# A gated recurrence over 512 steps: a block of probe instructions placed behind the last step

## The chip, the cores and the metric

The kernel runs on one core of one Trainium2 chip. The metric is the device time of one execution in microseconds; lower is better. Within the core, TensorE multiplies matrices (in the profile PE, and PEld for its weight loads), VectorE (DVE), ScalarE (ACT) and GpSimd (POOL) work elementwise, and SyncE (SP) issues transfers.

## The reference

For each of 512 time steps, with a state `h` of 8 rows by 512 and an input `x_t` of the same shape:

```python
def step(h, x_t):
    fused = sigmoid(concatenate([x_t, h], -1) @ w_W + w_b)
    hidden_state, output_state = split(fused, 2, -1)
    memory_state = x_t @ wx_W + wx_b + hidden_state * (h @ wh_W + wh_b)
    h_new = output_state * h + (1.0 - output_state) * tanh(memory_state)
    return h_new, h_new
out = x + scan(step, cond_1024, x)
```

Everything is float32. Step t+1 needs the `h` of step t, so the 512 steps run one behind the other.

## The kernel before

The 512 units of the state lie as 128 partitions by 4 chunks. All weights stay in SBUF: `wx` (line 118) for the input's part, `wgr` (line 122) and `whh` (line 125) for the state's part. `head` (line 92) holds the first half chunk of x and the first state. The order of instructions is the order of the program text (`tc.manual_schedule()`, line 170); on each engine they run in that order, and semaphores carry the dependences between engines.

Each step `i` of the loop at line 258 does this:

- TensorE, through the helper `mm` (line 177; every product has line 178 in the profile): 48 products of the state with the weights, each a fp32 stationary of 128x32 and a moving operand of 128x128, in the order of `ORDER` (line 27). The four output quarters `32*j` are taken in turn, so that four products run side by side in the four column groups of the array. The results add up in the PSUM banks R, G and H. Then `take(later, 1)` issues a quarter of the input's products for a coming group of four steps (`prefill`, line 215), into one of the two PSUM tiles `xps` (line 175).
- VectorE: 32x32 block transposes out of the banks (`turned`, line 301, recorded at line 303; `turn_h`, line 320), scans that form the gate sums and the new state (`scans`, line 280), and three one-column memsets of `idle` (line 383).
- ScalarE: sigmoids and tanh (`act`, line 204), and the copies that spread the input's part into the banks (`spread`, line 227) and write the bias (`seed`, line 211).
- GpSimd: the residual sum into `ot` (`add`, line 384), and SyncE: the store of 16 steps at a time (`store`, line 392).

The last step stands apart (lines 400 to 403): GpSimd adds one half (line 361), VectorE adds the other (`add(1, nc.vector)`, recorded at line 385), and SyncE stores the last four steps (line 395). Nothing follows.

Of the kernel before, what the change touches and what calls it, by code (L numbers as in the profile page):

```python
# [7 lines left out]
F32 = mybir.dt.float32  # L8
BF16 = mybir.dt.bfloat16
AF = mybir.ActivationFunctionType  # L10
ALU = mybir.AluOpType
PSUM = bass.MemoryType.PSUM

P = 128
NQ = 4
# [21 lines left out]
def tile_cond_rnn_residual(  # L37
# [39 lines left out]
    nc = tc.nc  # L77
# [4 lines left out]
    const = ctx.enter_context(tc.tile_pool(name="const", bufs=1))  # L82
# [9 lines left out]
    head = const.tile([P, NX + NQ * B], F32, name="head")  # L92
# [12 lines left out]
    def x_of(c, k, t, n):  # L105

        e, t = divmod(t, TC // 2)
        if c == 0 and e == 0:
            first = head[:, :NX].rearrange("p (k n) -> p k n", k=NQ)
            return first[:, k, t * B : (t + n) * B]  # L110
        return xins[c][:, e, k, t * B : (t + n) * B]
# [6 lines left out]
    wx = const.tile([P, NQ, NQ, 384], F32, name="wx")  # L118
# [6 lines left out]
    whh = const.tile([P, NQ, NQ, 128], F32, name="whh")  # L125
# [22 lines left out]
    zeros = const.tile([P, 512], F32, name="zeros")  # L148
# [14 lines left out]
    idle = const.tile([P, IDLE], F32, name="idle")  # L163

    def state(hf, i, slot=2):

        s = i % GS
        return hT[hf][i % NH][:, B * s : B * s + B, :, slot]
# [6 lines left out]
    xps = [psum.tile([P, 512], F32, name=f"xp{q}") for q in range(2)]  # L175

    def mm(out_, lhsT, rhs, start=False):
        nc.tensor.matmul(  # L178
            out_, lhsT, rhs, start=start, stop=False, skip_group_check=True
        )  # L180
# [11 lines left out]
    bias = const.tile([P, 512], F32, name="bias")  # L192
# [65 lines left out]
    for i in range(T):  # L258
        g, s = divmod(i, GS)
        c, t = divmod(i, TC)  # L260
# [6 lines left out]
        for n in (ORDER if i else FIRST).split():  # L267
# [3 lines left out]
            bank, k = n[0], int(n[1])  # L271
# [112 lines left out]
        def add(hf, engine):  # L384
            return engine.tensor_tensor(  # L385
                ot[:, t, 2 * hf : 2 * hf + 2, :].rearrange("p c n -> p n c"),
                x_of(c, slice(2 * hf, 2 * hf + 2), t, 1).rearrange("p c n -> p n c"),
                state(hf, i + 1),
                ALU.add,
            ).ins  # L390

        def store(t0):

            n = NQ * B
            nc.sync.dma_start(
                out=out[c][:, n * t0 : n * (t + 1)],
                in_=ot[:, t0 : t + 1].rearrange("p t k b -> p (t k b)"),
            )

        if i == T - 1:  # L400
            add(1, nc.vector)
            store(TC - LAST)
            continue
        for hf in (1, 0):
# [77 lines left out]
```

## Time and profile before

| what | value |
|---|---|
| times of the two runs | 1693.63 and 1693.91 us, median 1693.77 us |
| span of the profiled execution | 1691.7 us |
| what lies around the span, against the two runs | 1.93 to 2.21 us, 2.07 us against the median |
| PE busy | 1680.3 us, 99% of the span |
| DVE busy | 1087.0 us, 64% |
| ACT busy | 915.5 us, 54% |
| POOL busy | 231.2 us, 14% |
| last DMA issue on SP | at 1689.14 us, for 0.33 us |
| `out_dram<-ot` of 192 KB and 256 KB, issue to landing | 1.9 and 3.3 us |

The profiled execution's own time outside the profiler isn't listed apart from these runs; its span stands beside them, and the difference is taken as what lies around it. A group's line in the profile gives the engine, the operation, the tiles out<-in, the shape, how often it ran, the busy time and the mean of one in ns, and the idle time of the engine ahead of it. The timeline gives start, duration, engine, operation and how many instructions are merged into a line.

### The profile page before, as it was taken

The page shows a single profiled execution, that of the slowest core. Times are in us where ns is not written, and L with a number is a line of the kernel's source. Part 1 is how long each engine was busy: PE and PEld are TensorE (multiplying, and loading weights), DVE is VectorE, ACT ScalarE, POOL GpSimd, SP SyncE. Part 2 cuts the span into 40 slices and gives each one's busy share as a digit, 9 for nine tenths or more (in the row PEclk, how much of TensorE's full clock was granted, in tenths as well). Part 3 has the DMA queues.
Part 4 walks back from the last instruction along what each step waited for, and adds up shares of the span by engine and source line. Part 5 has one row for each costly group of instructions (what it writes and reads, how often), then busy time and mean ns, then how long its engine had stood idle before and what let it go on. Part 6 is the DMA issues. An engine that isn't in the chain of part 4 may idle for free.

```text
span 1691.7 us, 121258 instructions
## 1 busy us (share of the span) xinstructions
PE 1680.3 (99%) x53230; PEld 1467.6 (87%) x53230; DVE 1087.0 (64%) x8229; ACT 915.5 (54%) x5121; POOL 231.2 (14%) x1032
## 2 busy tenths in 40 slices
PE   8999999999999999999999999999999999999998
PEld 6888888888888888888888888888888888888887
DVE  5666666666666666666666666666666666666666
ACT  3555555555555555555555555555555555555554
POOL 0111111111111111111111111111111111111111
PEclk9999999999999999999999999999999999999999
DMA  4000000000000000000000000000000000000000
GB/s 177 17 17 5 17 17 17 17 4 17 17 17 17 4 17 17 17 17 13 9 18 17 17 17 4 17 17 17 17 5 17 17 17 17 4 17 11 11 11 10
DMA packets 11483, 30.86 MB, mean 18 GB/s; under 512 B 1220, under 2 KB 1732, under 8 KB 10952
## 3 DMA queue, kind: packets, MB, share of 16 engines
q1 hardware_dynamic: 10800, 22.94, 3.9%
q8 instruction: 416, 6.82, 1.7%
q14 instruction: 115, 0.94, 0.2%
q10 hardware_dynamic: 152, 0.16, 0.0%
HBM read 14.70 MB, written 8.39 MB: 14 GB/s over the span
## 4 chain that ended last, share of the span: by engine, by line
PE 98%; DMA 1%; DVE 0%; ACT 0%; issue 0%; SPq 0%
PE R L178 26%; PE G L178 26%; PE H L178 26%; PE xp L178 19%; DMA whh<-in_whh_dram 1%; DMA head<-in_xh_dram 0%; DVE md1A L321 0%; DVE hTA L283 0%; ACT hd0A L205 0%; ACT hTA L205 0%; SPq L124 0%; DVE tz L303 0%; ACT hTB L205 0%; DVE hTB L283 0%; ACT hd0B L205 0%
## 5 line engine op out<-in xcount | busy, mean ns | idle before, releaser
L178 PE MATMUL xp<-wx,xin 128*32 128x384 f32 x4032 | 431.3, 486 | 0.0
L178 PEld LDWEIGHTS R<-wgr,hTA 128*32 128x32 f32 x8176 | 247.4, 135 | 206.8 <-DVE hTA L283 206.4
L303 DVE STREAM_TRANSPOSE tr<-R 128x64 f32<-128x64 f32 x1022 | 194.4, 229 | 309.1 <-PE R L178 309.1
L178 PE MATMUL R<-wgr,hTA 128*32 128x128 f32 x8176 | 330.9, 273 | 2.2 <-DVE hTA L283 2.2
L178 PE MATMUL H<-whh,hTA 128*32 128x128 f32 x8192 | 331.3, 273 | 0.8 <-DMA whh<-in_whh_dram 0.8
L178 PE MATMUL H<-whh,hTB 128*32 128x128 f32 x8192 | 331.2, 273 | 0.0
L178 PE MATMUL R<-wgr,hTB 128*32 128x128 f32 x8176 | 330.6, 273 | 0.0
L178 PE MATMUL G<-wgr,hTB 128*32 128x128 f32 x8176 | 330.6, 273 | 0.0
L178 PE MATMUL G<-wgr,hTA 128*32 128x128 f32 x8176 | 330.6, 273 | 0.0
L385 POOL TENSOR_TENSOR ot<-xin,hTB 128x16 f32<-128x16 f32 x503 | 126.4, 251 | 1415.6 <-DVE hTB L283 1324.0
L205 ACT ACTIVATE hd0B<-tz 128x16 f32<-128x16 f32 x512 | 114.9, 224 | 305.3 <-DVE tz L303 305.3
L205 ACT ACTIVATE md0A<-tr 128x16 f32<-128x16 f32 x512 | 119.6, 234 | 265.2 <-DVE tr L303 265.2
L178 PEld LDWEIGHTS H<-whh,hTA 128*32 128x32 f32 x8192 | 260.2, 136 | 1.2 <-DMA whh<-in_whh_dram 1.2
L178 PEld LDWEIGHTS G<-wgr,hTA 128*32 128x32 f32 x8176 | 259.8, 136 | 0.0
L178 PEld LDWEIGHTS H<-whh,hTB 128*32 128x32 f32 x8192 | 254.5, 122 | 0.0
L178 PEld LDWEIGHTS G<-wgr,hTB 128*32 128x32 f32 x8176 | 254.1, 122 | 0.0
L178 PEld LDWEIGHTS R<-wgr,hTB 128*32 128x32 f32 x8176 | 245.2, 122 | 0.0
L283 DVE TENSOR_TENSOR_SCAN hTA<-hd0A,hTA 128x48 f32<-128x48 f32 x512 | 132.1, 258 | 149.2 <-ACT hTA L205 149.2
L283 DVE TENSOR_TENSOR_SCAN hTB<-hd0B,hTB 128x24 f32<-128x24 f32 x1024 | 158.1, 196 | 104.0 <-ACT hTB L205 104.0
L205 ACT ACTIVATE hd0A<-tz 128x16 f32<-128x16 f32 x512 | 118.9, 232 | 111.4 <-DVE tz L303 111.4
L321 DVE STREAM_TRANSPOSE md1A<-G 128x64 f32<-128x64 f32 x511 | 156.8, 307 | 28.7
L205 ACT ACTIVATE hTB<-hTB 128x16 f32<-128x16 f32 x512 | 121.2, 237 | 81.1 <-DVE hTB L283 80.5
(62 smaller groups left out, 1680.2 us busy)
## 6 DMA issues: line engine op xcount, KB each, us to landing
xin<-in_x_dram SPq DMA_DIRECT2D x31, 256.0 KB, 3.8
out_dram<-ot SPq DMA_DIRECT2D x31, 256.0 KB, 3.3
wx<-in_wx_dram SPq DMA_DIRECT2D x4, 768.0 KB, 7.2
wgr<-in_wgr_dram SPq DMA_DIRECT2D x4, 512.0 KB, 9.7
whh<-in_whh_dram SPq DMA_DIRECT2D x1, 768.0 KB
whh<-in_wh_dram SPq DMA_DIRECT2D x1, 256.0 KB, 11.2
out_dram<-ot SPq DMA_DIRECT2D x1, 192.0 KB, 1.9
head<-in_xh_dram ACTq DMA_DIRECT2D x1, 144.0 KB, 5.2
```

The lines of the kernel that those rows point to most:

```text
L178: nc.tensor.matmul(out_, lhsT, rhs, start=start, stop=False, skip_group_check=True)
L205: inst = nc.scalar.activation(out_, in_, func, **kw).ins
L283: nc.vector.tensor_tensor_scan(*[t_[:, :, c_].rearrange("p n c s -> p (n c s)") for t_ in (out_, d0, d1)], 0.0, ALU.mult, ALU.add,)
L303: inst = nc.vector.transpose(t_.rearrange("p c n -> p (c n)"), raw[n][hf]).ins
L321: nc.vector.transpose(md1[hf][g % 2][:, :, :, 0].rearrange("p n c -> p c n"), raw["h"][hf])
L385: return engine.tensor_tensor(ot[:, t, 2 * hf : 2 * hf + 2, :].rearrange("p c n -> p n c"), x_of(c, slice(2 * hf, 2 * hf + 2), t, 1).rearr ...
```

## The change

A function `measure()` is defined in the loop body and called once, in the last step, behind `add(1, nc.vector)` and ahead of `store`. It issues, in this order:

- VectorE: two copies of `whh` into the bf16 tile `bw` (1536 elements in each partition, the first 384 of a chunk repeated four times) and one copy of 96 elements of `head` into `st`. `top` and `top2` are views of `st` as bf16, 24 columns each.
- TensorE: nine groups of products into `xps`, with a one-column VectorE copy out of PSUM (`bar`) behind each: 120 bf16 products of 24 stationary columns (24 + 24 + 24 of width 128, 16 of width 64, 16 of 256, 16 of 384), 16 fp32 of 8 stationary columns and width 64, 16 of width 128, and 16 fp32 of full 128x128 by 128.
- VectorE: three memsets of 640 columns; 15 transposes from PSUM in five output layouts; 6 reductions, 9 scans and 6 small elementwise operations in threes; a chain of six dependent operations.
- ScalarE: six operations; GpSimd: three; then six VectorE operations that read what these two wrote, the last into `idle`.

None of its results reach the output. `rep` and `parts` are defined and not called. A built program's instruction lists show the new rows of every engine behind all of its rows of the loop, and the rows in front unchanged; SyncE's rows stay as they were, and the last store waits for the same GpSimd and VectorE sums. The bf16 products stand as a weight load and a product, two instructions each; a fp32 product is one instruction. No further table load is on ScalarE. Line numbers from 404 on are those of the changed kernel.

```diff
+        def measure():
+            bw = const.tile([P, 2, NQ, 384], BF16, name="bw")
+            for k in range(2):
+                nc.vector.tensor_copy(bw[:, k], whh[:, k, :, :].rearrange("p j n -> p (j n)")[:, :384].unsqueeze(1).broadcast_to([P, NQ, 384]))
+            st = const.tile([P, 96], F32, name="bst")
+            nc.vector.tensor_copy(st, head[:, :96])
+            top = st[:, :72].bitcast(BF16)[:, 5:144:6]
+            top2 = st[:, :72].bitcast(BF16)[:, 1:48:2]
+            a_, b_ = xps
...
+            def bar(t_):
+                nc.vector.tensor_copy(idle[:, :1], t_[:, :1])
+            def part(k, j, p, n=128, w=1):
+                return bw[:, k, j, n * p : n * (p + w)]
...
+            for k in range(2):
+                for j in range(NQ):
+                    for p in range(3):
+                        mm(b_[32 * j : 32 * j + 24, 0:128], top, part(k, j, p), start=k + p == 0)
+            bar(b_)
+            for k in range(2):
+                for p in range(3):
+                    for j in range(NQ):
+                        mm(a_[32 * j : 32 * j + 24, 0:128], top, part(k, j, p), start=k + p == 0)
+            bar(a_)
+            for p in range(3):
+                for k in range(2):
+                    for j in range(NQ):
+                        mm(b_[32 * j : 32 * j + 24, 0:128], top2, part(k, j, p))
+            bar(b_)
+            for k in range(2):
+                for n in range(2):
+                    for j in range(NQ):
+                        mm(a_[32 * j : 32 * j + 24, 0:64], top, part(k, j, n, 64))
+            bar(a_)
...
+                        mm(b_[32 * j : 32 * j + 24, 0:256], top, part(k, j, 0, 128, 2))
...
+                        mm(a_[32 * j : 32 * j + 24, 0:384], top, bw[:, k, j])
...
+                        mm(b_[32 * j : 32 * j + 8, 0:64], st[:, 0:24:3], whh[:, k, j, :64])
...
+                        mm(a_[32 * j : 32 * j + 8, 0:128], st[:, 0:24:3], whh[:, k, j, :128])
+            bar(a_)
+            for k in range(2):
+                for j in range(NQ):
+                    for n in range(2):
+                        nc.tensor.matmul(b_[:, 0:128], wx[:, k, j, :128], wx[:, k, j, 128:256], start=False, stop=False, skip_group_check=True)
+            bar(b_)
+            u = const.tile([P, 640], F32, name="bu")
+            nc.vector.memset(u, 0.0)
...
+            V = nc.vector
+            tp = a_[:, 0:64]
+            for _ in range(3):
+                V.transpose(v[:, 0:64], tp)
+            for _ in range(3):
+                V.transpose(v[:, 0:80].rearrange("p (c b s) -> p c s b", c=2, s=5)[:, :, :4], tp)
+            for _ in range(3):
+                V.transpose(v[:, 0:80].rearrange("p (c b s) -> p c b s", c=2, s=5)[:, :, :, :4], tp)
+            for _ in range(3):
+                V.transpose(v[:, 0:80].rearrange("p (s c b) -> p c s b", c=2, s=5)[:, :, :4], tp)
+            for _ in range(3):
+                V.transpose(v[:, 0:128], a_[:, 0:128])
+            for _ in range(3):
+                V.tensor_reduce(w_[:, 0:16], v[:, 0:80].rearrange("p (c s b) -> p c b s", c=2, s=5), mybir.AxisListType.X, ALU.add)
+            for _ in range(3):
+                V.tensor_reduce(w_[:, 0:32], v[:, 0:160].rearrange("p (c s b) -> p c b s", c=4, s=5), mybir.AxisListType.X, ALU.add)
+            for _ in range(3):
+                V.tensor_tensor_scan(w_[:, 0:80], u[:, 0:80], v[:, 0:80], 0.0, ALU.mult, ALU.add)
...
+            for _ in range(3):
+                V.tensor_tensor(w_[:, 0:48:3], u[:, 0:48:3], v[:, 0:48].bitcast(BF16)[:, 1:96:6], ALU.subtract)
+            V.tensor_tensor(w_[:, 0:16], u[:, 0:16], v[:, 0:16], ALU.mult)
+            V.tensor_tensor(w_[:, 16:32], w_[:, 0:16], v[:, 0:16], ALU.mult)
+            V.tensor_tensor(w_[:, 32:48], w_[:, 16:32], v[:, 0:16], ALU.mult)
+            V.tensor_tensor_scan(w_[:, 64:112], u[:, 0:48], w_[:, 0:48], 0.0, ALU.mult, ALU.add)
+            V.tensor_tensor(w_[:, 128:144], w_[:, 64:80], v[:, 0:16], ALU.mult)
+            V.tensor_reduce(w_[:, 144:160], w_[:, 128:144].unsqueeze(2).broadcast_to([P, 16, 4]), mybir.AxisListType.X, ALU.add)
+            nc.scalar.activation(u[:, 256:288].rearrange("p (c b) -> p c b", c=4), w_[:, 0:128].rearrange("p (c n) -> p c n", c=4)[:, :, :8], AF.Sigmoid)
+            nc.scalar.activation(u[:, 288:304], w_[:, 0:16], AF.Tanh)
+            nc.scalar.activation(u[:, 320:352], w_[:, 0:32], AF.Sigmoid)
+            nc.scalar.activation(u[:, 352:480], a_[:, 0:128], AF.Identity, bias=zeros[:, :1])
+            nc.scalar.copy(b_[:, 0:128], zeros[:, 0:128])
+            nc.scalar.copy(b_[:, 0:64], zeros[:, 0:64])
+            nc.gpsimd.tensor_tensor(u[:, 512:528], w_[:, 0:16], v[:, 0:16], ALU.mult)
...
+            nc.vector.tensor_tensor(w_[:, 0:64], u[:, 256:320], u[:, 512:576], ALU.mult)
...
+            nc.vector.tensor_tensor(idle[:, :1], w_[:, 72:73], zeros[:, :1], ALU.add)
+
         if i == T - 1:
             add(1, nc.vector)
+            measure()
             store(TC - LAST)
             continue
```

## The prediction, made before the run

> **What bounds the kernel now.** I read the page first, then the end of the timeline, since the change sits behind the last step, then the groups for durations, and last the start of the timeline, the only place with bf16 products and a long idle of TensorE.
>
> ```profile
> span 1691.7 us, 121258 instructions
> ```
>
> ```profile
> PE 98%; DMA 1%; DVE 0%; ACT 0%; issue 0%; SPq 0%
> ```
>
> The first line is the span; the second, from the chain of work that ended last, gives TensorE 98% of it. The loop is TensorE's time, and the change touches no row in it. What matters is what stands behind TensorE at the end:
>
> ```profile
> 1686.48 0.62 PE L178 MATMUL H<-whh,hTA 128*32 128x128 f32 x16
> 1686.73 0.31 DVE L321 STREAM_TRANSPOSE md1A<-G 128x64 f32<-128x64 f32 x1
> 1686.92 0.62 PE L178 MATMUL H<-whh,hTB 128*32 128x128 f32 x16
> 1687.08 0.22 DVE L283 TENSOR_TENSOR_SCAN m<-md0A,md1A 128x32 f32<-128x32 f32 x1
> ...
> 1688.88 0.19 DVE L385 TENSOR_TENSOR ot<-xin,hTB 128x16 f32<-128x16 f32 x1
> 1689.14 0.33 SPq L395 DMA_DIRECT2D out_dram<-ot  x1
> ```
>
> TensorE is done at 1687.54. VectorE's last work ends at 1688.88 + 0.19 = 1689.07. The store is issued at 1689.14, and the span ends at 1691.7, so the last 2.6 us are the store alone. The scan m at 1687.08 waits for md1A, a VectorE result that ends at 1687.04: a VectorE instruction that depends on one before it starts about 0.04 to 0.06 us behind its end. I use 0.05.
>
> The groups that give prices (lines picked from all over the list of groups, shapes kept apart):
>
> ```profile
> L283 DVE TENSOR_TENSOR_SCAN hTA<-hd0A,hTA 128x48 f32<-128x48 f32 x512 | 132.1, 258 | 149.2 <-ACT hTA L205 149.2
> L283 DVE TENSOR_TENSOR_SCAN m<-md0A,md1A 128x32 f32<-128x32 f32 x512 | 115.0, 225 | 0.0
> L321 DVE STREAM_TRANSPOSE md1B<-H 128x64 f32<-128x64 f32 x512 | 115.7, 226 | 0.4 <-PE H L178 0.4
> L235 DVE STREAM_TRANSPOSE md1B<-xp 128x32 f32<-128x32 f32 x256 | 49.1, 192 | 0.0
> L160 DVE MEMSET hTA<- 128x192 f32 x8 | 1.7, 218 | 0.0
> L193 DVE COPY bias<-xp 128x512 f32<-128x512 f32 x1 | 0.7, 692 | 1.3 <-PE xp L178 1.3
> L149 DVE MEMSET zeros<- 128x512 f32 x1 | 0.5, 485 | 0.1
> L196 DVE COPY hTB<-head 128x16 f32<-128x16 f32 x2 | 0.3, 176 | 0.0
> L321 DVE STREAM_TRANSPOSE md1A<-xp 128x64 f32<-128x64 f32 x1 | 0.3, 255 | 0.0
> L385 DVE TENSOR_TENSOR ot<-xin,hTB 128x16 f32<-128x16 f32 x1 | 0.2, 189 | 0.0
> ```
>
> Scans cost (258 - 225)/16 = 2.06 ns a column, memsets (485 - 218)/320 = 0.834. And TensorE's timeline, its start and a stretch near the end:
>
> ```profile
> 2.15 0.31 PE L178 MATMUL G<-none 128*128 128x128 bf16 x1
> 2.26 0.31 PE L178 MATMUL H<-none 128*128 128x128 bf16 x1
> 2.69 3.52 PE L178 MATMUL xp<-zeros 128*128 128x512 f32 x4
> 6.77 1.10 PE L178 MATMUL xp<-rows,ones 128*128 128x512 f32 x2 [0.57 <-DVE hTB L160]
> ```
>
> ```profile
> 1661.47 0.86 PE L178 MATMUL xp<-wx,xin 128*32 128x384 f32 x8
> 1662.12 0.65 PE L178 MATMUL R<-wgr,hTA 128*32 128x128 f32 x16
> ```
>
> After 2.07 us of idle, bf16 products of 128 columns start 0.107 us apart, and fp32 records of 512 columns take 3.52/4 = 0.88; from 6.77 on, two of them fit in 1.10. So the array starts at half its later rate, though the granted clock of those windows reads 1.00.
>
> **The change part by part.** Nothing is removed or moved; SP's and the loop's rows stay. The block is behind VectorE's sum of line 385 and no earlier: TensorE's first new weight load waits for a VectorE copy that stands behind that sum, and ScalarE's and GpSimd's first new rows wait for VectorE too. So the block starts at 1689.07, beside the store. The store waits for the sum alone and is covered: its 2.6 us is no longer the end.
>
> *Copies* (on the path: TensorE waits). 1536 columns by the memset slope, since that row too stays in SBUF: 218 + 1344 x 0.834 = 1339 ns, twice is 2.68; the copy of 96 columns 0.17 + 80 x 0.0008 = 0.24; handover 0.05. Sum 2.97. Ends: 0.17 each, as for 16 columns (-2.3); by the slope of the copy from PSUM, (692 - 173)/496 = 1.05 ns a column, 1.76 each (+0.8).
>
> The Trainium skill ("VectorE: DVE Perf Modes", the perf-mode tier table) gives fp32 copies within SBUF two columns a cycle at 0.96 GHz. Estimated from it the two copies take 1.9 together, and the total falls by 0.8.
>
> *TensorE.* In a column group a quarter of the input's products (8 records of 384 columns, 0.65 us to the next group at 1662.12) is 2 records per column group, so 0.85 ns a column and record; a fp32 product has two records. The start shows a bf16 record at half the fp32 price per column (0.107/128 against 0.88/512), so 54 ns for 128 columns. In rotation over four groups, steady pairs of load and product come 0.437/16 = 27.3 ns apart (H at 1686.48 and 1686.92); I take that as the floor. First group, three in a row on one column group: 24 x 54 = 1.30. Two more of 24: 1.31. Widths 64 and 256: 16 x 27.3 = 0.44 each. Width 384: 163/4 = 41, 0.65. fp32 of 64: 0.44; of 128: 0.87; the full array, without rotation, 16 x 2 x 109 ns = 3.49. Sum 8.94, plus 0.19 for the last to drain (0.62 - 0.437): 9.13. The bars alternate between two banks, so each is covered by the next group; only the ninth is not. Ends: below, the array alone instead of the 27.3 ns floor (13.6 ns a pair for 128 columns, 6.8 for 64), 1.0 less; above, half rate (next) and the slow pairs among the rivals.
>
> *Half rate.* TensorE now idles from 1687.54 to 1692.04, 4.5 us; the longest idle that kept the rate in this trace is 0.78 us, so no row decides it. Cold throughout adds 1.30 + 0.43 + 0.65 + 0.44 + 0.87 + 3.49 = 7.2. Warm again after some 4 us, as at the start, it adds 1.30 in the first group and little in the others, which the 27.3 ns floor sets. I take 0 and keep 1.3 and 7.2.
>
> The Trainium skill ("TensorE: Matmul & The Clock Gate", Part 1) says that an idle window of about 3.4 us halves the array's clock and as long a busy one restores it. By that rule the gap is long enough, and the total rises by about 1.3.
>
> *Ninth bar and memsets.* One PSUM column, bounded by the 32-column transpose, 0.19 with handover; 640 columns 485 + 128 x 0.834 = 592 ns, three 1.78. Sum 1.97. All on the path: VectorE is in order.
>
> *VectorE's chain*, each with a wait on VectorE itself. Transposes: three of 64 columns at 0.22 (md1B's 0.226), nine with strided output at 0.255 (the 64-column one without products beside it), three of 128 at 0.29: 3.83; ends for the nine, the 0.207 of tz and the 0.307 of md1A beside products, -0.4 and +0.5. Reductions, no row: elementwise 0.189 plus 1.06 ns for each further input (the transposes' slope, (226 - 192)/32), 0.256 for 80 and 0.34 for 160, 1.79 in all; ends 1.1 (flat 0.189) and 2.5 (a scan's slope). Scans of 80, 64, 48: 0.324, 0.291, 0.258, three each, 2.62. Six elementwise 1.13. The chain of six: 4 x 0.189 + 0.258 + 0.24 = 1.25. Handover 42 x 0.05 = 2.1. Sum 12.72; if they overlapped as the independent ones do (two transposes tr in 0.38), 5 less.
>
> *ScalarE and GpSimd*: ScalarE's first two take 0.36 (0.13 apart, 0.23 long) behind the scan of the chain, whose two followers take 0.53; GpSimd's three take about 0.7 behind the chain's first product, which has 1.3 behind it. Cost 0; without that cover 0.4.
>
> *Last six*: three of 64 columns at 0.24, three at 0.19, six handovers: 1.59.
>
> *End*: the span ran some 0.33 to 0.66 past the store's landing (1689.14 or 1689.47 plus 1.9); I take 0.3 behind VectorE.
>
> Sum 2.97 + 9.13 + 1.97 + 12.72 + 1.59 = 28.4, so VectorE ends at 1717.5 and the span at 1717.8, 26.1 more. Around the span I keep 2.07, what the median of the two runs (1693.77) has over it: 1719.9, plus 1.5%.
>
> **The rivals.**
> *Slower by over 2%: bf16 pairs issue one instruction at a time.* A bf16 product is two instructions, a fp32 one is one, and one fp32 instruction per 54.6 ns is the fastest issue that the trace shows. At 109 a pair, 120 pairs take 13.1 in place of 4.14: +9.0, 1728.9. It decides from some 100 ns a pair (7.7 more). For: the only bf16 pairs in the trace are 107 ns apart. Against: that is also the half rate for 128 full columns, and weight load and product records flow at 27.3.
> *Cold array*: +1.3 to +7.2, 1721 to 1727, still within 2%.
> *Cheap VectorE*: instructions overlap and copies run at twice the slope: 5 + 1.3 less, 1713.6.
> *No effect*: the block hides beside the store. Only 2.6 us are there, and the block's first copies fill them; that needs a block 26 us shorter. Against: every bar waits for TensorE, and all rows are in the built program. 1693.8.
>
> **How the numbers follow.** Forecast 0.58, cold array 0.20, cheap VectorE 0.08, slow pairs 0.13, no effect 0.01. The point is the forecast's 1719.9. The range runs from cheap VectorE, 1713, to the slow pairs' edge at 1729. Two per cent of 1693.77 is 33.9 us, about what a measurement of this kernel can tell from no change; only the slow pairs cross it (1727.6), with a little from a cold array with long handovers: slower 0.15, same 0.84, faster 0.01.
>
> **What would show it.** The loop's rows end at 1689.1 as now; the store lands inside the block; VectorE's new rows follow each other at duration plus 0.05; the copies of line 405 at 1.3; bf16 groups of 24 at 0.65 to 1.3, the full array at 3.5. A TensorE block of over 16 us, handovers of over 0.2, or a longer loop would prove me wrong.

## The result and the profile after

The changed kernel takes 1719.36 us (median of two runs, 1719.32 to 1719.40) against 1693.77: ratio 1.0151, 95% interval 1.0122 to 1.0181. It is slower by 25.6 us, 1.5%: the whole interval lies above 1 and below the 2% that the prediction took as an edge. The forecast was 1719.9 with a range of 1713 to 1729. The profiled span is 1717.6 us, forecast 1717.8.

The page's span, and its shares of the chain that ended last, by engine:

```profile
span 1717.6 us, 121774 instructions
```

```profile
PE 97%; DVE 1%; DMA 1%; ACT 0%; issue 0%; SPq 0%
```

VectorE has come into the chain with 1%: the block. The timeline of the changed kernel from the last step on (start, duration, engine, operation, how many; left-out rows are marked by three dots):

```profile
1687.13 0.62 PE L178 MATMUL H<-whh,hTB 128*32 128x128 f32 x16
...
1689.11 0.19 DVE L385 TENSOR_TENSOR ot<-xin,hTB 128x16 f32<-128x16 f32 x1
1689.21 1.82 DVE L405 CAST bw<-whh 128x1536 bf16<-128x1536 f32 x2
1689.36 0.33 SPq L395 DMA_DIRECT2D out_dram<-ot  x1
...
1691.20 4.20 PE L178 MATMUL xp<-bw,bst 128*24 128x128 bf16 x120 [3.45 <-DVE bst L407]
...
1695.21 1.51 PE L178 MATMUL xp<-whh,bst 128*8 128x64 f32 x64
...
1696.66 3.84 PE L467 MATMUL xp<-wx 128*128 128x128 f32 x32
...
1700.53 0.16 DVE L416 COPY idle<-xp 128x1 f32<-128x1 f32 x1 [3.58 <-PE xp L467]
1700.77 0.59 DVE L470 MEMSET bu<- 128x640 f32 x1
...
1702.63 0.76 DVE L478 STREAM_TRANSPOSE bv<-xp 128x64 f32<-128x64 f32 x3
1703.42 0.96 DVE L480 STREAM_TRANSPOSE bv<-xp 128x64 f32<-128x64 f32 x3
1704.42 0.82 DVE L482 STREAM_TRANSPOSE bv<-xp 128x64 f32<-128x64 f32 x3
...
1714.90 0.22 DVE L506 TENSOR_REDUCE bz<-bz 128x16 f32<-128x64 f32 x1
...
1716.47 0.16 DVE L521 TENSOR_TENSOR idle<-bz,zeros 128x1 f32<-128x1 f32 x1
```

The loop ends as before: VectorE's sum at line 385 ends at 1689.30 (1689.07 before). The store is issued at 1689.36, beside the copies, and lands inside the block. From there the work goes down one line: copies, TensorE, the ninth bar, memsets, VectorE's chain. TensorE's first product carries the wait that the copies cost it, 3.45 us of idle. VectorE's last instruction ends at 1716.63, 0.97 ahead of the end of the span.

The granted clock in stretches of the changed kernel (stretch and length, then busy time and instructions of PE, PEld, DVE, ACT and POOL, then the clock):

```profile
1691.20:1691.48 0.28, 0.28 (x19) 0.28 (x23) 0.00 (x0) 0.00 (x0) 0.00 (x0) 0.99 0.00 0
1691.48:1694.89 3.41, 3.38 (x110) 2.83 (x102) 0.79 (x5) 0.00 (x0) 0.00 (x0) 0.50 0.02 5
1694.89:1696.60 1.71, 1.71 (x76) 1.46 (x68) 0.31 (x2) 0.00 (x0) 0.00 (x0) 1.00 0.00 0
```

The array did fall to half rate, from 1691.48 for 3.41 us, after its first 19 products. In the single starts of the trace, four bf16 pairs of 128 columns come 56 ns apart ahead of 1691.48 and 107 ns after. So the bf16 groups took their 4.0 us for another reason than the forecast gave; the experiments take the two apart.

### The profile page after: what moved, and what is told of

Read it like the earlier page. It is cut to its first block, busy times and chain, and to the rows that moved or that the text cites. A ratio compares the mean times of both kernels' runs of the same rounds, so it can differ in the third digit from the quotient of the medians.

```text
span 1717.6 us, 121774 instructions
## 1 busy us (share of the span) xinstructions
PE 1689.3 (98%) x53446; PEld 1472.1 (86%) x53446; DVE 1105.4 (64%) x8292; ACT 918.9 (54%) x5127; POOL 230.2 (13%) x1035
## 3 DMA queue, kind: packets, MB, share of 16 engines
q8 instruction: 417, 6.83, 1.6%
## 4 chain that ended last, share of the span: by engine, by line
PE 97%; DVE 1%; DMA 1%; ACT 0%; issue 0%; SPq 0%
PE R L178 26%; PE G L178 26%; PE H L178 26%; PE xp L178 19%; DMA whh<-in_whh_dram 1%; DMA head<-in_xh_dram 0%; PE xp L467 0%; DVE md1A L321 0%; DVE hTA L283 0%; ACT hd0A L205 0%; ACT hTA L205 0%; DVE bz L490 0%; DVE bz L492 0%; DVE bv L486 0%; DVE bw L405 0%
```

## The experiments

All eight kernels keep the loop and the store as they are, and the block's results reach no output. Each was run four times, the changed kernel twice. Beside four of them (four fillers, one column group, the block that ends at the ninth bar, the moved memsets) the kernel before took 1693.97 us, beside the other four 1693.76, so a difference from the changed kernel's 1719.36 is good to some 0.2 us. Where the runs of one kernel lie further apart than that, the reading goes by the profiled stretch.

**TensorE kept busy through the copies.**

```diff
+            for _ in range(8):
+                mm(xps[1], zeros[:, :128], zeros)
             bw = const.tile([P, 2, NQ, 384], BF16, name="bw")
```

> Eight fp32 products of zeros, 128x128 by 512, stand on TensorE ahead of the block, so that it works through VectorE's copies and has no idle of 3.45 us. They add into a PSUM tile and change nothing in it. Theory (the idle halves the array's rate, and the rate is what priced the bf16 groups): the granted clock stays at 1.00, four bf16 pairs of 128 columns come some 55 ns apart instead of 107, the bf16 groups take 2.0 to 2.3 us instead of 4.0, and the time falls by 1.5 to 2.0 us to about 1717.5. Rival (27.3 ns a pair is a floor of issue, as the prediction had it): the groups keep 4.0 us and the time stays at 1719.4, or rises by up to 0.3 for the last filler product.

1721.44 us. The filler was mis-sized: a fp32 product of 512 columns is two records, and eight products ran 7.13 us, so the block's products began at 1694.55, 3.35 later. The clock stayed at 1.00 and the bf16 groups took 2.70 us (1694.55 to 1697.25). That speaks for the clock, but 2.70 lies outside the expected 2.0 to 2.3, and the total says little. The same with four products:

> Four products of zeros instead of eight ahead of the block: a fp32 product of 512 columns proved to take two records of 0.44 us, so four fill 3.5 us, the length of VectorE's copies, and TensorE neither idles nor delays the block. Theory (half the rate comes from the idle of 3.45 us): the clock stays at 1.00, the bf16 groups take 2.7 us as behind eight fillers and not 4.0, and the time falls by 1.3 us to 1718.1. Rival (what gained in the run with narrow copies was the copies alone): the time stays at 1719.4.

1717.94 us, 1.42 below the changed kernel. Three of the four runs lie between 1717.83 and 1717.97; the fourth took 1719.71, but its span is 1716.4 us against 1716.0 to 1716.2, so most of its surplus lies around the span. The stretch of the bf16 groups in this kernel's clock view:

```profile
1690.90:1693.66 2.76, 2.63 (x122) 2.31 (x124) 0.79 (x5) 0.00 (x0) 0.00 (x0) 1.00 0.03 6
```

Full clock, 2.72 us from 1690.94 to 1693.66. The idle cost 1.3 us through the clock (4.01 us without the fillers), and the rival falls. In the single starts, four pairs of 128 columns come 56 ns apart all along, 14 ns a pair, so the forecast's floor of 27.3 ns a pair doesn't exist.

**Copies a quarter as wide.** Every bf16 product reads the one part.

```diff
-                nc.vector.tensor_copy(bw[:, k], whh[...].unsqueeze(1).broadcast_to([P, NQ, 384]))
+                nc.vector.tensor_copy(bw[:, k, 0], whh[...])
```

> The two copies into bw take 384 columns in place of 1536, and every bf16 product reads that one part; results of the block differ, which nothing reads. Theory (copies within SBUF run two columns a cycle, 0.95 us for 1536, and the array's rate falls only for an idle of a whole window of about 3.4 us): a copy takes 0.33 to 0.36, TensorE idles about 2.3 us, the clock stays at 1.00, the bf16 groups take 2.0 to 2.3 us, and the time falls by 1.2 + 1.9 = 3.1 us to 1716.3. Rival A (any idle beyond 0.8 us halves the rate): clock at 0.50 in the groups, time falls by 1.2 to 1718.2. Rival B (floor of issue): clock at 1.00, groups still 4.0 us, 1718.2.

1716.93 us, 2.43 less. The copies in the list of groups (busy time and mean ns of one), the changed kernel first, then the narrow copies:

```profile
L405 DVE CAST bw<-whh 128x1536 bf16<-128x1536 f32 x2 | 1.8, 952 | 0.0
```

```profile
L405 DVE CAST bw<-whh 128x384 bf16<-128x384 f32 x2 | 0.6, 353 | 0.0
```

(952 - 353)/1152 = 0.52 ns a column, half of the 1.05 that the copy from PSUM had in the profile of before and less than the memsets' 0.834. TensorE idled 2.24 us, kept its clock, and needed 2.71 us for the bf16 groups: the copies gave 1.2 us and the clock 1.3. The expected 3.1 was too much because TensorE runs into two bars, each of which reads the PSUM tile that a later group writes. In the single starts, the third group's first lies 0.17 us behind the second's last, at 1690.80, and the first bar ends at 1690.75; the fifth group's first lies 0.32 us behind the fourth's last, at 1691.58, and the third bar ends at 1691.53. In the changed kernel the wait ahead of the fifth group was there already (0.28 us), the one ahead of the third is new (0.04 us there). Without the two the groups would take 2.71 - 0.17 - 0.32 = 2.2 us, an estimate within the expected 2.0 to 2.3.

In the profiled run neither rival holds: the clock was 1.00, against rival A, and the groups took 2.71 us and not 4.0, against rival B. But one of the four runs took 1718.19 us, 1.2 to 1.4 above the others and just what rival A gives, at a mean granted clock of 0.995 where they have 0.996. The run on one column group, below, shows what can make such a difference.

**No products.** The nine groups and their bars are cut out.

```diff
-            for k in range(2):
-                for j in range(NQ):
-                    for p in range(3):
-                        mm(b_[32 * j : 32 * j + 24, 0:128], top, part(k, j, p), start=k + p == 0)
-            bar(b_)
...
             u = const.tile([P, 640], F32, name="bu")
```

> All nine groups of products and the bars behind them are left out. If the block is one chain through VectorE, the time falls by the stretch from TensorE's first product (1691.20) to the end of the last bar (1700.69): 9.5 us, to 1709.9, and VectorE's rows behind keep their durations. If part of the products lies beside VectorE's work, it falls by less, down to 5.

1709.96 us, 9.40 less (runs from 1709.87 to 1710.38). VectorE's rows follow the copies at once (the first memset at 1691.27) with durations unchanged. Nothing of the products lay beside VectorE's work.

**The threes write to three places in turn.**

```diff
-            for _ in range(3):
-                V.transpose(v[:, 0:64], tp)
+            for r in range(3):
+                o = 160 * r
+                V.transpose(v[:, o : o + 64], tp)
...
```

> The eleven threes of VectorE (transposes, reductions, scans, elementwise) write to three places in turn instead of one, so that none of the three depends on the one before it. Theory (an instruction that doesn't depend on the last one starts before that ends, as the two transposes tr do in the loop, 0.38 us for two of 0.228): spacing falls by some 0.08 to 0.11 us for each second and third of a three, 1.8 to 2.4 us in all, to about 1717.3. Rival (instructions on VectorE follow each other end to end with or without a wait, and what the wait costs is only the 0.02 to 0.03 us seen between them): the time falls by at most 0.6 us, to 1718.8.

1714.69 us, 4.67 less: twice what the theory gave, and far from the rival. Two of the four runs took 1714.11 and 1714.25, the other two 1715.13 and 1715.32 at a granted clock of 0.995 in place of 0.997. The timeline of this kernel, its first threes (start, time from the first's start to the last's end):

```profile
1702.59 0.44 DVE L479 STREAM_TRANSPOSE bv<-xp 128x64 f32<-128x64 f32 x3
1702.95 0.52 DVE L482 STREAM_TRANSPOSE bv<-xp 128x64 f32<-128x64 f32 x3
1703.35 0.47 DVE L485 STREAM_TRANSPOSE bv<-xp 128x64 f32<-128x64 f32 x3
```

A three of transposes now takes 0.36 to 0.40 from its start to the next one's, where the changed kernel has 0.79 to 1.00 (1702.63, 1703.42, 1704.42 in its timeline). The expectation speaks of eleven threes; there are twelve, 36 instructions (15 transposes, 6 reductions, 9 scans, 6 elementwise). It counted the second and third of each three; the first also overlaps the three before it. In the two profiles, from the first three's start to the start of the row behind the last, the stretch falls from 11.14 us (1702.63 to 1713.77) to 5.89 (1702.59 to 1708.48), by 5.25/36 = 0.15 us an instruction; by the medians it is 4.67/36 = 0.13. What a dependence (here two writes to one place) costs on VectorE is then the whole overlap, of which only 0.03 to 0.04 us shows as a gap between rows.

**All of the first group on one column group**, upon the kernel with narrow copies.

```diff
-                        mm(b_[32 * j : 32 * j + 24, 0:128], top, part(k, j, p), start=k + p == 0)
+                        mm(b_[0:24, 0:128], top, part(k, j, p), start=k + p + j == 0)
```

> On the kernel with narrow copies, whose array runs at the full rate: all 24 products of the first group go to the output rows 0 to 23, one column group, in place of three in a row on each of four. Theory (each column group has its own line of work, and the array starts what stands behind in another group early, so only products of one column group wait for each other): the 24 starts take 24 x 53 ns = 1.28 us instead of 0.36, and the time rises by 0.9 over the narrow copies' 1716.9, to 1717.8. Rival (the pairs flow at 14 ns wherever they go): 0.36 us, 1716.9.

1719.36 us in the median, but the four runs are 1719.34, 1717.74, 1719.56 and 1719.37. The profiled one is the first; its clock view:

```profile
1690.16:1690.92 0.76, 0.76 (x14) 0.76 (x15) 0.00 (x0) 0.00 (x0) 0.00 (x0) 1.00 0.30 86
1690.92:1694.34 3.42, 3.36 (x90) 3.22 (x91) 0.63 (x4) 0.00 (x0) 0.00 (x0) 0.50 0.02 5
```

At full clock 14 products start in 0.76 us, 56 ns apart in the single starts behind the first, against 19 in 0.28 us, 15 ns each, when three in a row go to each of four column groups (the changed kernel). The theory of separate lines holds, and the rival falls.

But here the rate halved at 1690.92, behind an idle of only 2.24 us (1687.92 to 1690.16), while the profiled run with narrow copies alone kept its rate behind an idle as long (1687.71 to 1689.95). The clock's record tells the two apart. In all ten profiles every stretch at one rate, from change to change, is a whole number of times 3.413 us (493 to 498 times for the long one of the loop), so the rate is set anew on a fixed grid of windows of that length. The windows around the idle, those with narrow copies alone first, then the one here:

```profile
1685.82:1689.24 3.42, 1.89 (x72) 1.63 (x64) 2.18 (x17) 1.72 (x10) 0.69 (x3) 1.00 0.02 5
1689.24:1692.65 3.41, 2.58 (x120) 2.31 (x124) 1.45 (x8) 0.01 (x1) 0.00 (x0) 1.00 0.08 24
```

```profile
1687.51:1690.92 3.41, 1.17 (x30) 0.92 (x23) 2.06 (x15) 1.18 (x7) 0.24 (x1) 1.00 0.07 19
```

With narrow copies alone a boundary of the grid splits the idle, and TensorE is busy for 55% and 76% of the two windows. Here the idle lies within one window, TensorE is busy for 34% of it, and the next window runs at half rate. It is the same in all ten profiles: behind a window at full rate in which TensorE was busy for 41% or less, half rate follows, and behind one of 55% or more, full rate; none lies between. So where the grid falls is enough to tell these two apart, and the single column group need not be a cause. The loop ends at another place of the grid in each run: the first full-rate stretch starts between 5.24 and 8.15 us into the span.

The run of 1717.74 is the expected 1717.8. It has no trace, but its mean granted clock is 0.996 and that of the other three 0.995, and 3.41 us at half rate take 0.001 off that mean; so it most likely kept its rate.

**A block that ends at the ninth bar.**

> The block ends behind the ninth bar; memsets, VectorE's chain, and ScalarE's and GpSimd's new rows are left out. The last VectorE instruction should end at 1700.7. Theory (a fixed close of some 0.95 us stands between the last engine's work and the end of the span, whatever came last): span 1701.6, and the time falls by 16.0 to 1703.4. Rival (a close of 0.3, as the prediction took it, and the other 0.65 belongs to the chain's last instructions): span 1701.0, time 1702.8.

1703.85 us, runs from 1703.17 to 1704.26. In the profiled run (span 1702.5) the array was at half rate for 6.83 us instead of 3.41, two windows of the grid (1689.84 to 1696.67): in the first TensorE was busy for 63%, which didn't bring the full rate back, in the second for 99%, which did. So the ninth bar is late (the bar in its timeline):

```profile
1701.43 0.16 DVE L416 COPY idle<-xp 128x1 f32<-128x1 f32 x1 [3.58 <-PE xp L467]
```

It ends at 1701.59, the span 0.9 behind it. In the changed kernel it was 0.97, behind another instruction of the same engine. So a close of 0.9 to 1.0 us stands behind VectorE's last work, whichever instruction that is, and the rival (0.3) falls; a kernel that ends on another engine was not run. Before the change the close stood behind the store. The expected total was missed by 0.45 in the median, and by 0.86 in the profiled run, whose bar ends 0.89 later than the expected 1700.7.

**The memsets moved ahead of the ninth bar.**

```diff
-            bar(b_)
             u = const.tile([P, 640], F32, name="bu")
             nc.vector.memset(u, 0.0)
...
+            bar(b_)
             V = nc.vector
```

> The three memsets of 640 columns stand ahead of the ninth bar instead of behind it, where VectorE waits 3.58 us for the full-array products. Theory (VectorE's order alone put them on the path): the stretch from the ninth bar to the first transpose loses the memsets' 1.9 us, and the time falls by as much to 1717.5. Rival (memsets that run beside the products slow them, or the bar is late): a fall of less than 1 us.

1717.62 us, 1.74 less (runs from 1717.30 to 1718.50). The timeline of this kernel around the bar:

```profile
1697.36 0.59 DVE L469 MEMSET bu<- 128x640 f32 x1
...
1700.86 0.16 DVE L416 COPY idle<-xp 128x1 f32<-128x1 f32 x1 [1.56 <-PE xp L467]
1700.94 0.81 DVE L478 STREAM_TRANSPOSE bv<-xp 128x64 f32<-128x64 f32 x3
```

From the bar's start to the first transpose it is 0.08 us where it was 2.10 (1700.53 to 1702.63). The full-array products take the same 3.84 us. Same instructions, under a cover that was there: free. That the total fell by less than these 2.02 us fits the clock: the half-rate window came later here (from 1692.70) and took in the fp32 products ahead of the full array, 1.96 us in place of 1.45, while the bf16 groups took 3.71 in place of 4.01.

None of these beats the kernel before, and none can, as all of them add work behind its end.

## Why the prediction came out right

Point by point, forecast against the changed kernel's profile:

| term | forecast us | measured us | from |
|---|---|---|---|
| end of VectorE's last sum | 1689.07 | 1689.30 | line 385 |
| copies, to TensorE's first product | 2.97 | 1.90 | 1689.30 to 1691.20 |
| products | 9.13 | 9.30 | to 1700.50 |
| of these, bf16 groups | 4.14 | 4.01 | 1691.20 to 1695.21 |
| ninth bar and memsets | 1.97 | 2.21 | to 1702.71 |
| VectorE's chain | 12.72 | 12.41 | to 1715.12 |
| last six | 1.59 | 1.51 | to 1716.63 |
| end of the span | 0.3 | 0.97 | to 1717.6 |
| around the span | 2.07 | 1.76 | 1719.36 - 1717.6 |

The frame held: one line of work behind line 385, nothing of it hidden, the store covered, ScalarE and GpSimd covered (VectorE's wait ahead of line 516 is 0.12 us). Cutting the products took away 9.40 us, almost the 9.5 of their stretch. What the forecast leaned on most, nearest rows for VectorE, held too: the scans were 0.324, 0.291 and 0.257 us against 0.324, 0.291 and 0.258, the memsets 592 ns as worked out. Reductions were dearer (0.294 and 0.436, forecast 0.256 and 0.34), handovers cheaper (0.03 to 0.04, forecast 0.05).

Four terms were wrong and cancelled. That the total came within 0.54 us of the forecast is luck: copies and floor were priced too high, half rate and end too low.

- *Copies*: by the memset slope 1.34 us each, measured 0.952. The memset was the wrong nearest row. The Trainium skill's two columns a cycle ("VectorE: DVE Perf Modes", the perf-mode tier table) is what the trace shows, 0.52 ns a column.
- *Half rate*: I took 0 and it happened, at 1.3 us (2.7 to 4.0), the lower of the two prices that I kept; but that price was worked out from the first group alone, and what slowed down was the bf16 products from about the twentieth on. The Trainium skill's window ("TensorE: Matmul & The Clock Gate", Part 1) fits the length of the stretch at 0.50, 3.41 us.
- *The floor of 27.3 ns a pair* was read off fp32 products that fill their column groups: the spacing there is the array's time, not an issue limit. The forecast didn't keep to its own floor either: it priced the fp32 products of width 64, 32 records, at 0.44 us, 14 ns each, and they took 0.45. At full rate a pair takes 14 ns. At half rate it takes 107/4 = 26.7, so the floor's price and the half rate's price are the same number, and each error paid for the other. *First group* on top: I priced three in a row on one column group as serial, 1.30, but its 24 starts were all out within 0.43 us, because the other column groups start early, as the run on one column group bears out.
- *End*: 0.97 in place of 0.3. I had subtracted a landing of 1.9 us, which is the row of the 192 KB store; the last one is of 64 KB and lands in 1.5 us, which leaves 0.7 to 1.1 of close in the profile of before too.

Had TensorE stayed at full rate, as with the four fillers (1717.94), the forecast would have been 2.0 us too high. The rival of slow pairs is refuted: 109 ns a pair was forecast there, 14 to 27 measured. The rival of a cheap VectorE is what a block without dependences does: 4.67 less by the run, 5 by the forecast. Here every row of VectorE's chain has a dependence, so that half of it didn't apply; its other half, cheaper copies, came true.

## What to carry to other kernels

Work appended behind the last step costs its whole length, less only the time that a store was alone at the end; price it instruction by instruction, and order it so that an engine does its independent part while it waits (1.74 us for moving three memsets). A spacing seen between instructions is a floor only if nothing else explains it: look whether the units behind it are full. On VectorE, let neighbours write to different places: the dependence costs the overlap, 0.13 to 0.15 us per instruction here, and the profile shows only 0.03 to 0.04 of it as a gap. And an idle of TensorE well below 3.4 us can halve its rate, if it leaves one window of the clock's grid mostly idle; as the grid falls elsewhere in each run, compare stretches of profiles, and not only medians, when an effect is of the size of 1.3 us.

## What the runs showed of the hardware

- TensorE's rate is set in windows of 3.413 us on a fixed grid. An idle of 3.44 to 3.46 us ahead of the products halved it in all four profiles that had one, for 3.41 us (once 6.83), and an idle of 2.24 us in one of two. The Trainium skill ("TensorE: Matmul & The Clock Gate", Part 1) tells of an idle window of about 3.4 us; here a window in which TensorE was busy for 41% was followed by half rate too, and one of 55% was not. What holds between the two stays open. At half rate a window of 63% didn't bring the full rate back, and one of 96% did. Runs of one and the same kernel differed by up to 1.9 us.
- Each column group of the array works through its own products: 56 ns a product of 128 bf16 columns in one group, 14 ns with four groups at the same clock, even if the program has three in a row for each.
- A close of 0.9 to 1.0 us stands between VectorE's last work and the end of the span (0.97 in the changed kernel, 0.9 in the block that ends at the ninth bar).
- What made the memsets of line 470 to 474 start 0.68 us apart at 0.59 us each, with no dependence between them in the kernel, stays open.
